# Attention's value products in quarters: one planner, two kinds of TensorE work, in a two-layer hybrid of convolution and attention

## The chip, the cores and the metric

The kernel runs on one core of one Trainium2 chip. The core has engines that work side by side, each on its own instruction queue: TensorE (PE, matrix products; its weight loads are listed apart as PEld), VectorE (DVE), ScalarE (ACT, here mostly exponentials), GpSimd (POOL) and SyncE (SP, which issues the transfers). An engine takes its instructions in the order in which they were written for it and waits, where it must, on semaphores that the others raise. The metric is the device time of one execution in microseconds (us); the median of three runs counts.

## The reference

Four images of 64 x 64 positions with 128 channels go through two layers. Cut to what matters here:

```python
# layer 0: elu, two 3x3 convolutions, a gate, causal attention with 1 head
# (4 wide for queries and keys, 16 wide for values), residual sums
x = _L0_conv_ref(x, ...)
# layer 1, on tokens t = [4, 4096, 128]
q = (x @ wq).reshape(bsz, seqlen, 16, 8)          # k, v alike
scores = einsum('bqhd,bkhd->bhqk', q, k)
probs = softmax(scores)
attn = einsum('bhqk,bkhd->bqhd', probs, v)
h = x + attn @ wo
t = t + h + (silu(h @ w1) * (h @ w3)) @ w2         # x is a layernorm of t
t = t + top-2 of 8 experts of layernorm(t), weighted by a router
```

The attention of layer 1 is the bulk: 4 batches x 16 heads x 4096 x 4096 scores, an exponential of each, and the product of the exponentials with the values.

## The kernel before

**Steps and turns.** Attention of layer 1 is cut into *segments*: one batch, one group of four heads, one tile of 512 queries (`Segment`, L1340). A segment runs over 32 key tiles of 128 keys; one key tile is a *step* (`attention_step`, L910). A step has two halves. `scores()` issues four products on PE, one per head, each on its own 32 rows of the array, into two score tiles `s` in PSUM (three such tiles exist, L192), and two exponentials on ACT from `s` into tiles `e` (six exist, L188). `values(es)` issues four products of 9 output rows (the sum of the exponentials and the 8 value channels) by 512 queries, which add up in the one PSUM tile `acc` over the segment's key tiles. At the last key tile DVE copies `acc` to `at`, and SP writes it to DRAM. In the trace each of these fp32 products stands as two instructions, so that a step's values show as `x8`.

**The planner.** The main loop (from L1476) issues one step per *turn* and writes the order of every engine by hand: `InOrder` (L104) ties each instruction to the one before it on its engine. It keeps account of PE's time with a few prices in us:

```python
    EXPS, SCORES, VALUES, PIECE, AHEAD = 1.81, 0.43, 0.987, 0.446, 0.39
        left = ahead + EXPS - SCORES - (VALUES if len(undone) > 2 else 0.0)
        ahead = min(max(left, 0.0), AHEAD)
        finish(2)
```

`EXPS` is the time that a turn has (its two exponentials), `left` what PE has over. A turn first issues its scores (`do_step`, L289), then perhaps other work, and last the values that are two steps behind: the list `undone` holds the steps whose values are outstanding, and `finish(2)` (L293, L1521) issues the oldest until two are left. What is left over, up to `AHEAD`, is carried into the next turn.

**The other work of a turn** comes from two sources.

- *Fillers* (`insert`, L307, and `advance`, L298): generators that do all the rest of the network in small pieces, between attention's steps. `convolutions` (L529) and `first_attention` (L666) prepare the next batch; `second_operands` (L742) makes queries, keys and values of layer 1; `last_part` (L1087) does everything behind attention for one tile of 512 tokens (output product, feed-forward part, router, experts), 32 of them in all. A piece is mostly half of a product of 512 columns (`halves`, L374: 256 columns, four products of 32 rows), or two products of 128 columns. A generator yields a price and a word: "held" if the single PSUM bank `m` (L194) is only half written, "free" or "stop" otherwise. A second piece then ends the bank in the next turn, and DVE reads it.
- *DVE jobs* (`Beside`, L958): in each segment over all keys, key tile 20 gets its exponentials from DVE. A job issues four score products into the bank `m` (a `unit` each, L986), DVE works out a polynomial (`beside_work`, L1037) into tiles `ey`, and two half products of 256 queries (`half`, L1026) add the result to `acc`.

In the kernel before a turn takes at most one of these: a filler piece or a piece of a job, when `left` is at least `PIECE`, or when a credit for fillers (which spreads them over the steps that remain) or the job's due time asks for it. The first two turns of a segment take none (`quiet`). `dve_time` (L150) estimates when DVE reads the bank (`turn_at[0] + 1.1` for a tile in `m`), and the loop uses that estimate to see whether the bank is empty.

**The end.** When the steps are used up, `finish(0)` issues the values that are left, and `run_alone` (L1250) runs what is left of the fillers with the PSUM banks of the scores. The last of them is `last_part` of the last tile of the last batch: it can begin only when that tile's attention is written to DRAM. It reads it back through `operands` (L1051): the sums (`sums<-d_a`), the rest (`an<-d_a`), then after a reciprocal `d_r<-sums` and `per<-d_r`.

Of the kernel before, what the change touches and what calls it, by code (L numbers as in the profile page):

```python
# [15 lines left out]
P = 128  # L16
# [4 lines left out]
QB = 512  # L21
# [5 lines left out]
SLOT = 32  # L27
NSLOT = P // SLOT
# [4 lines left out]
NH1, HD1 = 16, 8  # L33
# [93 lines left out]
def fast_path(ctx: ExitStack, tc: tile.TileContext, a: dict, where: dict, out: bass.AP, verdict):  # L127
# [11 lines left out]
    turn_at, dve_at, pool_at, bank_at = [0.0], [0.0], [0.0], [0.0]  # L139
# [5 lines left out]
            took = 0.65 + 1.25e-3 * int(np.prod(aps[0].shape[1:]))  # L145
            pool_at[0] = max(pool_at[0], turn_at[0] + 0.5) + took

    power_at, before = [0.0], [None]

    def dve_time(name, args):  # L150

        aps = [x for x in args if hasattr(x, "shape")]

        def reads(prefix):
            return any(x.name.startswith(prefix) for x in aps[1:])

        from_bank = reads("m_") or any(x.name == "m" for x in aps[1:])
        in_sbuf = not any(x.space == bass.MemoryType.PSUM for x in aps)
        took = max(int(np.prod(x.shape[1:])) for x in aps[:2]) / 960.0
        if in_sbuf and name in ("tensor_scalar", "tensor_copy"):  # L160
            took *= 0.5
        took += 0.075
        if any(x.name == before[0] for x in aps[1:]):
            took += 0.117
        before[0] = aps[0].name
        begins = 0.0
        if from_bank:
            begins = turn_at[0] + 1.1
        elif reads("acc"):
            begins = turn_at[0] + 1.85  # L170
        elif reads("e_"):
            begins = turn_at[0] + 2.2
        elif reads("rs_") and name == "tensor_scalar":
            begins = power_at[0] + 1.3
        begins = max(dve_at[0], begins)
        if in_sbuf and begins < pool_at[0] - 0.2:
            took += 0.75
        dve_at[0] = begins + took
        if aps[0].name.startswith("ve_"):
            power_at[0] = dve_at[0]  # L180
        if from_bank:
            bank_at[0] = dve_at[0]
# [96 lines left out]
    acc = ps_o.tile([P, QB], FP, tag="acc", name="acc")  # L279
# [6 lines left out]
    steps_in, undone, fillers = [], [], []  # L286
    bank_held = [False]

    def do_step(step):  # L289
        scores, values = step  # L290
        undone.append((values, scores()))

    def finish(leave):  # L293
        while len(undone) > leave:
            values, es = undone.pop(0)
            values(es)

    def advance(part):  # L298

# [7 lines left out]
    def insert():  # L307

        while fillers:
            r = advance(fillers[0])  # L310
            if r is not None:
                return r[0]
            fillers.pop(0)
        return 0.0
# [519 lines left out]
    def first_step(c, r, qx0, sums, found):  # L834

        diagonal = r == c

        if diagonal and c > 0:
            place = [(0, 0, 0), (1, P, P), (0, QB, 2 * P), (1, QB, 3 * P)]
            spans = [(0, QB + 2 * P), (P, QB + P)]  # L840
        else:
            place = [(j % 2, (j // 2) * QB, 0) for j in range(NSLOT)]
            spans = [(0, 2 * QB)] * 2

        def scores():
            ss, es = [s_tile(), s_tile()], [e_tile(), e_tile()]
            for j in BY_TILE:
                half, lo, off = place[j]
                r_ = slice(j * SLOT, j * SLOT + n_row)
                pe.matmul(  # L850
                    ss[half][:, lo : lo + QB - off],
                    lhsT=kx0[r_, r, :].bitcast(FR),
                    rhs=qx0[r_, off:].bitcast(FR),
                    start=True,
                    stop=True,
                )
            for e, s, (lo, hi) in zip(es, ss, spans):
                act.activation(e[:, lo:hi], s[:, lo:hi], AF.Exp)
            parts = []
            for j, (half, lo, off) in enumerate(place):  # L860
                e = es[half][:, lo : lo + QB - off]
                if diagonal:
                    at = j * P - off
                    if at:
                        pool.memset(e[:, :at], 0.0)
                    dve.tensor_tensor(e[:, at : at + P], e[:, at : at + P], k_of["tri"], ALU.mult)
                parts.append((off, e))
            return parts

        def values(parts):  # L870
            if r == 0:
                sums.append(acc if alone[0] else m_tile())
            for j, (off, e) in enumerate(parts):
                pe.matmul(
                    sums[0][j * SLOT : (j + 1) * SLOT, off:],
                    lhsT=v0[:, 4 * r + j, :],
                    rhs=e,
                    start=r == 0,
                    stop=r == c,
                )  # L880
            if r == c:
                at = chunk("at0")
                dve.tensor_copy(at, sums[0])
                found.append(at)

        return scores, values


    def keys(d, g, quarter, place):
# [20 lines left out]
    def attention_step(b, seg, kt, place, qx, vg, part):  # L910
        g, c = seg.g, seg.c

        def scores():
            ss, es = [s_tile(), s_tile()], []
            for j in BY_TILE:
                r = slice(j * SLOT, (j + 1) * SLOT)
                pe.matmul(
                    ss[j % 2][:, (j // 2) * QB : (j // 2 + 1) * QB],
                    lhsT=kx[r, place * P : (place + 1) * P].bitcast(FR),
                    rhs=qx[r, :].bitcast(FR),  # L920
                    start=True,
                    stop=True,
                )
            for s in ss:
                e = e_tile()
                act.activation(e, s, AF.Exp)
                es.append(e)
            return es

        def values(es):  # L930
            if kt == seg.hi - 1:
                beside_rest(seg)
            for j in range(NSLOT):
                pe.matmul(
                    acc[j * SLOT : j * SLOT + 1 + HD1, :],
                    lhsT=vg[:, kt // 4, kt % 4, j, :],
                    rhs=es[j % 2][:, (j // 2) * QB : (j // 2 + 1) * QB],
                    start=kt == seg.lo,
                    stop=kt == seg.hi - 1,
                )  # L940
            if kt == seg.hi - 1:
                at = chunk("at1")
                if part:
                    dve.tensor_tensor(at, acc, part[0], ALU.add)
                else:
                    dve.tensor_copy(at, acc)
                to = scratch[b]["a"][c, g] if seg.hi == NT else scratch[b]["p"][g, c]
                sp.dma_start(out=to, in_=at)
                if seg.hi == NT and g == NG1 - 1:
                    fillers.append([last_part(b, c), LAST, (b, c), False])  # L950
                    last_parts_left[0] -= 1

        return scores, values


    beside_todo = []
# [86 lines left out]
    def beside_rest(seg):  # L1043
        for job in seg.jobs:
            while job.halves < 2:
                beside_work(1e9)
                job.piece()
# [270 lines left out]
    lo, hi = where["rfold"]  # L1318
# [51 lines left out]
    jobs = []  # L1370
    now, quiet = [0], [False]
# [86 lines left out]
    def spread_beside():  # L1458
# [5 lines left out]
    left = run_alone(  # L1464
        [st.conv, first_attention(0, st), second_operands_beside(0, st), fold_and_spread(), spread_beside()],
        lambda: st.second >= plan[0].n and len(spread_of) == 3 and not st.plain,
    )
# [5 lines left out]
    credit, waiting = 0.0, False  # L1473


    EXPS, SCORES, VALUES, PIECE, AHEAD = 1.81, 0.43, 0.987, 0.446, 0.39  # L1476
    ahead = 0.0
    while True:
        turn_at[0] += EXPS
# [21 lines left out]
            later = PREPARE * (B - len(batches)) + LAST * (last_parts_left[0] - 1)  # L1501
            rate = (sum(part[1] for part in fillers) + later) / max(40, sum(steps_left) - 160)
        credit = min(3.0, credit + rate)
        left = ahead + EXPS - SCORES - (VALUES if len(undone) > 2 else 0.0)
        free = bool(fillers) and fillers[0][3]
        turn = not quiet[0] and free and not waiting
        if turn:
            took = insert()
            credit -= took
            left -= took  # L1510
        can = [job for job in jobs if job.can() and (left >= PIECE or job.late())]
        empty = bank_held[0] or bank_at[0] <= turn_at[0] + 0.3 or batches[b].second < NQ
        if can and empty and not (quiet[0] or bank_held[0] or steps_in or waiting):
            can[0].piece()
            left -= PIECE
        elif not turn and (waiting or not quiet[0] and empty and credit > 0.0 and (left >= PIECE or credit > 1.5)):
            took = insert()
            credit -= took
            left -= took
        ahead = min(max(left, 0.0), AHEAD)  # L1520
        finish(2)  # L1521
        for job in jobs:
            job.step()
        beside_work(turn_at[0] + 2.9, any(job.age > 3 * job.units + 4 for job in jobs if job.halves < 2))
# [720 lines left out]
```

## Time and profile before

| what | value |
|---|---|
| runs | 7981.13, 7985.75, 7992.59 us; median 7985.75 |
| profiled execution, its own time | 7983.82 us |
| its span, first to last instruction | 7982.0 us |
| TensorE clock granted, mean | 0.992 |
| first and last exponential of attention (start) | 71.6 and 7905.5 us |
| exponentials `e<-s` | 8256 |
| products `s<-qx,f_kx` of 512 columns, mean length | 495 ns |
| products `acc<-e,vg` of 512 columns, mean length | 594 ns |

The profile is one execution. A group line names the engine and operation, the tile written and those read, the shape, the count, then the busy time and the mean length of one, then the idle time before them and what ended it. On the timeline the first column is the start in us, the second how long the merged instructions lasted together. Products on PE are pipelined: a bar reaches into the next ones, so that the distance between starts, not the length, says how long PE was taken. Share of span in the chain of waits that ended last:

```profile
PE 87%; issue 7%; DVE 3%; ACT 1%; DMA 1%; POOL 1%; SPq 0%; ACTq 0%; DVEq 0%; POOLq 0%
PE acc L114 42%; PE s L114 26%; PE m L114 18%; DVE ey L114 1%; ACT e L114 1%; DVE h L114 0%; SPq L114 0%; DVE t L114 0%; DMA blocks<-d_y 0%; DMA f_kx<-d_k 0%; DVE em L114 0%; DVE pos L114 0%; DVE at L114 0%; POOL rs L114 0%; DVE c L114 0%
```

All instructions stand under L114, the line of the helper that records them; they are told apart by their tiles.

### The profile page before, as it was taken

To read this page: it belongs to the slowest core of one execution; us is meant where nothing else is said; L and a number is where in the kernel's file an instruction comes from. 1 tells how busy PE (TensorE), PEld (TensorE's weight loads), DVE (VectorE), ACT (ScalarE), POOL (GpSimd) and SP (SyncE) were. 2 spreads that over 40 slices of the span, in tenths; PEclk is the share of its full clock that TensorE was granted. 3 is DMA by queue.
4 is the path that set the end of the run, shared out by engine and by line. 5 is a ranking of instruction groups with operands and counts; after the bars stand their busy time and mean duration, and the time that the engine had idled before them with its cause. 6 is when DMAs were issued, how large, how long until landed. Compare 5 with 4: busy or idle time off the path is not lost.

```text
span 7982.0 us, 177748 instructions
## 1 busy us (share of the span) xinstructions
PE 7822.9 (98%) x73601; PEld 2457.5 (31%) x73601; DVE 4810.9 (60%) x9289; ACT 7670.4 (96%) x8459; POOL 676.4 (8%) x592
## 2 busy tenths in 40 slices
PE   7999999999999999999999999999999999999998
PEld 3232232332332323333332323333333333333333
DVE  4333556463666766665657766665666666666666
ACT  1899999999999999999999999999999999999996
POOL 1201211000012110000002111000000000000000
PEclk9999999999999999999999999999999999999998
DMA  2221010111110111111010111111111111111221
GB/s 73 67 69 68 22 60 30 61 35 59 35 31 13 51 39 45 33 38 37 28 35 25 34 32 39 51 43 33 32 31 50 51 51 50 54 49 51 68 72 42
DMA packets 332343, 356.58 MB, mean 45 GB/s; under 512 B 146083, under 2 KB 222339, under 8 KB 331523
## 3 DMA queue, kind: packets, MB, share of 16 engines
q1 hardware_dynamic: 327507, 343.35, 13.8%
q8 instruction: 579, 9.49, 0.5%
q10 hardware_dynamic: 4016, 1.77, 0.1%
q14 instruction: 241, 1.97, 0.1%
HBM read 209.24 MB, written 135.79 MB: 43 GB/s over the span
## 4 chain that ended last, share of the span: by engine, by line
PE 87%; issue 7%; DVE 3%; ACT 1%; DMA 1%; POOL 1%; SPq 0%; ACTq 0%; DVEq 0%; POOLq 0%
PE acc L114 42%; PE s L114 26%; PE m L114 18%; DVE ey L114 1%; ACT e L114 1%; DVE h L114 0%; SPq L114 0%; DVE t L114 0%; DMA blocks<-d_y 0%; DMA f_kx<-d_k 0%; DVE em L114 0%; DVE pos L114 0%; DVE at L114 0%; POOL rs L114 0%; DVE c L114 0%
## 5 line engine op out<-in xcount | busy, mean ns | idle before, releaser
L114 ACT ACTIVATE e<-s 128x1024 f32<-128x1024 f32 x8256 | 7608.8, 1097 | 101.3 <-PE s L114 97.2
L114 PE MATMUL acc<-e,vg 128*9 128x512 f32 x31872 | 4220.1, 594 | 0.6 <-DVE at L114 0.5
L114 PE MATMUL s<-qx,f_kx 32*128 32x512 f32 (+1 forms) x16512 | 2659.5, 495 | 38.7 <-DMA f_kx<-d_k 19.2
L114 PEld LDWEIGHTS s<-qx,f_kx 32*128 32x128 f32 (+1 forms) x16512 | 1084.7, 181 | 3862.1 <-ACT e L114 3633.7
L114 PEld LDWEIGHTS acc<-e,vg 128*9 128x9 f32 x31872 | 727.0, 90 | 799.7 <-issue 407.1
L114 DVE SCALAR_TENSOR_TENSOR ey<-ey,eg 128x512 f32<-128x512 f32 x1344 | 949.5, 706 | 33.1
L114 PE MATMUL m<-v,f_wino 128*32 128x256 f32 x5376 | 430.9, 392 | 12.8 <-POOL v L114 7.3
L114 DVE COPY at<-acc 128x512 f32<-128x512 f32 x131 | 90.6, 691 | 549.3 <-PE acc L114 546.0
L114 DVE TENSOR_SCALAR ey<-m 128x512 f32<-128x512 f32 x448 | 308.0, 688 | 85.7 <-PE m L114 71.0
L114 DVE SCALAR_TENSOR_TENSOR ey<-ey,em 128x512 f32<-128x512 f32 x448 | 323.4, 722 | 10.7
L114 DVE TENSOR_TENSOR by_e<-m,gates 128x512 f32<-128x512 f32 x240 | 165.0, 688 | 272.3 <-PE m L114 268.9
L114 DVE SCALAR_TENSOR_TENSOR eg<-em,ey 128x512 f32<-128x512 f32 x448 | 315.0, 703 | 9.4
L114 POOL TENSOR_TENSOR rs<-ve,f_minus_half 128x4 f32<-128x4 f32 x64 | 65.2, 1019 | 2967.6 <-DVE ve L114 2967.6
L114 DVE SCALAR_TENSOR_TENSOR ey<-eg 128x512 f32<-128x512 f32 x448 | 308.0, 687 | 0.0
L114 PE MATMUL m<-f_we,y2T 128*32 128x256 f32 x3840 | 306.7, 391 | 0.0
L114 POOL TENSOR_TENSOR v<-r 128x1024 f32<-128x1024 f32 x112 | 217.9, 1951 | 997.8 <-PE m L114 997.3
L114 DVE COPY sd<-m 128x512 f32<-128x512 f32 x168 | 116.0, 691 | 271.7 <-PE m L114 271.1
L114 POOL TENSOR_TENSOR t<-t,h 128x512 f32<-128x512 f32 x32 | 50.2, 1569 | 2240.3 <-DVE h L114 2240.3
L114 PE MATMUL m<-hT,f_fw 128*32 128x256 f32 (+1 forms) x2728 | 236.1, 391 | 0.4
L114 DVE TENSOR_TENSOR t<-m,t 128x512 f32<-128x512 f32 x61 | 42.2, 692 | 275.0 <-PE m L114 275.0
L114 DVE TENSOR_SCALAR em<-ey 128x512 f32<-128x512 f32 x448 | 197.2, 440 | 14.0
L114 DVE TENSOR_SCALAR em<-em 128x512 int32<-128x512 int32 x448 | 195.8, 437 | 11.1
(260 smaller groups left out, 4384.8 us busy)
## 6 DMA issues: line engine op xcount, KB each, us to landing
f_kx<-d_k SPq DMA_DIRECT2D x139, 512.0 KB
qx<-d_q SPq DMA_DIRECT2D x152, 256.0 KB
d_q<-two SPq DMA_DIRECT2D x64, 512.0 KB
d_a<-at SPq DMA_DIRECT2D x128, 256.0 KB
vg<-d_v SPq DMA_DIRECT2D x32, 576.0 KB
d_k<-two SPq DMA_DIRECT2D x32, 512.0 KB
d_v<-vc SPq DMA_DIRECT2D x32, 288.0 KB
xe<-in_x_dram SPq DMA_DIRECT2D x32, 256.0 KB
```

The lines of the kernel that those rows point to most:

```text
L114: made = op(*args, **kw)
```

## The change

The values of a step become divisible. `attention_step` returns a third item, `early`, and its `values` takes a range of quarters: columns `begin * 128` to `end * 128` of the 512 queries, for all four heads. The first step of a segment stays whole, and the last step's quarters may go early only when the segment's DVE job has done both its halves. `undone` counts quarters (4 for a step), and `add_values` issues as many as it is asked for.

A turn now issues at its end the quarters beyond eight (`must`), and after them, while `left` holds the price of a quarter and more than six quarters are outstanding, single quarters of the oldest step: up to two, half of a step's values. The prices are new: scores 0.54, a quarter 0.218, a job's unit 0.23 (`HEAD`), and 0.2 at most is carried over. Every job may place a piece in a turn, not the first alone; a turn may hold two filler pieces where the first leaves the bank half written and `left` holds the second; and DVE's estimated start is shifted by the first one's price (`shift`). The order of scores, other work and values within a turn is as before.

```diff
@@ dve_time
-            begins = turn_at[0] + 1.1
+            begins = turn_at[0] + 1.1 + shift[0]
@@
     def do_step(step):
-        scores, values = step
-        undone.append((values, scores()))
+        scores, values, split = step
+        undone.append([values, scores(), 4, split])
+
+    def add_values(quarters):
+
+        while quarters > 0:
+            values, es, left, split = undone[0]
+            some = min(left, quarters) if split else left
+            values(es, *((4 - left, 4 - left + some) if split else ()))
+            quarters -= some
+            undone[0][2] -= some
+            if some == left:
+                undone.pop(0)
+
+    def behind():
+        return sum(step[2] for step in undone)
 
     def finish(leave):
-        while len(undone) > leave:
-            values, es = undone.pop(0)
-            values(es)
+        add_values(sum(step[2] for step in undone[: max(0, len(undone) - leave)]))
@@ attention_step
-        def values(es):
-            if kt == seg.hi - 1:
+        def values(es, begin=0, end=4):
+            if kt == seg.hi - 1 and begin == 0:
                 beside_rest(seg)
+            lo, hi = begin * P, end * P
             for j in range(NSLOT):
                 pe.matmul(
-                    acc[j * SLOT : j * SLOT + 1 + HD1, :],
+                    acc[j * SLOT : j * SLOT + 1 + HD1, lo:hi],
                     lhsT=vg[:, kt // 4, kt % 4, j, :],
-                    rhs=es[j % 2][:, (j // 2) * QB : (j // 2 + 1) * QB],
+                    rhs=es[j % 2][:, (j // 2) * QB + lo : (j // 2) * QB + hi],
                     start=kt == seg.lo,
-                    stop=kt == seg.hi - 1,
+                    stop=kt == seg.hi - 1 and end == 4,
                 )
-            if kt == seg.hi - 1:
+            if kt == seg.hi - 1 and end == 4:
                 at = chunk("at1")
...
-        return scores, values
+        def early():
+            return kt < seg.hi - 1 or all(job.halves == 2 for job in seg.jobs)
+
+        return scores, values, early if kt > seg.lo else None
@@ main loop
-    EXPS, SCORES, VALUES, PIECE, AHEAD = 1.81, 0.43, 0.987, 0.446, 0.39
+    EXPS, SCORES, VALUES, PIECE, HEAD, AHEAD = 1.81, 0.54, 0.218, 0.446, 0.23, 0.2
...
-        left = ahead + EXPS - SCORES - (VALUES if len(undone) > 2 else 0.0)
-        free = bool(fillers) and fillers[0][3]
-        turn = not quiet[0] and free and not waiting
-        if turn:
+        must = max(0, behind() - 8)
+        left = ahead + EXPS - SCORES - VALUES * must
+        took, beside = None, False
+        if not quiet[0] and fillers and fillers[0][3] and not waiting:
             took = insert()
             credit -= took
             left -= took
-        can = [job for job in jobs if job.can() and (left >= PIECE or job.late())]
         empty = bank_held[0] or bank_at[0] <= turn_at[0] + 0.3 or batches[b].second < NQ
-        if can and empty and not (quiet[0] or bank_held[0] or steps_in or waiting):
-            can[0].piece()
-            left -= PIECE
-        elif not turn and (waiting or not quiet[0] and empty and credit > 0.0 and (left >= PIECE or credit > 1.5)):
+        for job in jobs:
+            cost = HEAD if job.units < NSLOT else PIECE
+            if job.can() and empty and (left >= cost or job.late()):
+                if not (quiet[0] or bank_held[0] or steps_in or waiting):
+                    job.piece()
+                    left -= cost
+                    beside = True
+        for n in range(1 if waiting else 2):
+            if took is None:
+                go = waiting or not (quiet[0] or beside) and empty and credit > 0.0
+                go = go and (waiting or left >= PIECE or credit > 1.5)
+            else:
+                go = took > 0.0 and bank_held[0] and left >= PIECE
+            if not go:
+                break
+            shift[0] = 0.0 if took is None else took
             took = insert()
+            shift[0] = 0.0
             credit -= took
             left -= took
+        add_values(must)
+        while left >= VALUES and behind() > 6 and undone[0][3] and undone[0][3]():
+            add_values(1)
+            left -= VALUES
         ahead = min(max(left, 0.0), AHEAD)
-        finish(2)
```

Layer 0's attention steps (`first_step`, L834) return `None` as their third item and stay whole. Each output element is the same sum; only the place at which a DVE job's key tile is added among the others can differ. Neither a tile nor a buffer is added.

## The prediction

> **What bounds the kernel now.** I read the page first (busy time, the chain of waits), then the timeline of single engines.
>
> ```profile
> span 7982.0 us, 177748 instructions
> ...
> PE 7822.9 (98%) x73601; PEld 2457.5 (31%) x73601; DVE 4810.9 (60%) x9289; ACT 7670.4 (96%) x8459; POOL 676.4 (8%) x592
> ...
> L114 ACT ACTIVATE e<-s 128x1024 f32<-128x1024 f32 x8256 | 7608.8, 1097 | 101.3 <-PE s L114 97.2
> ```
>
> Two engines are nearly full at once. ACT's exponentials are the work nobody else can take; PE feeds them. The idle 101.3 us before the exponentials understate the loss, since a busy bar includes an exponential's latency. Pace tells more. The timeline of ACT alone:
>
> ```profile
> 6399.23 16.62 ACT L114 ACTIVATE e<-s 128x1024 f32<-128x1024 f32 x18
> 6415.49 0.46 ACT L114 ACTIVATE pr<-lg 128x32 f32<-128x32 f32 x1
> 6415.61 63.14 ACT L114 ACTIVATE e<-s 128x1024 f32<-128x1024 f32 x68
> 6478.63 0.63 ACT L114 ACTIVATE th<-h 128x512 f32<-128x512 f32 x1
> ```
>
> 18 exponentials take 6415.49 - 6399.23 = 16.26 us, 0.903 each: ACT's own pace, 1.806 for a turn's two. The 68 behind them take 63.02 us, 0.927 each: there ACT waits a little in every turn. Over the whole trace the 7,993 distances from one full exponential to the next hold 203 us above 0.903: 85.7 us in 3,341 distances of 0.915 to 0.96, 34 in 249 of 0.96 to 1.2, 81 in 57 longer ones. The first band is what a smoother PE could win back. PE's timeline shows its cause:
>
> ```profile
> 6405.61 0.70 PE L114 MATMUL s<-qx,f_kx 32*128 32x512 f32 x4
> 6406.24 1.04 PE L114 MATMUL acc<-e,vg 128*9 128x512 f32 x8
> 6407.22 0.92 PE L114 MATMUL s<-qx,f_kx 32*128 32x512 f32 x4
> ...
> 6411.73 0.43 PE L114 MATMUL m<-y2T,f_rw 128*32 128x128 f32 x8
> 6411.98 0.61 PE L114 MATMUL acc<-e,vg 128*9 128x512 f32 x4
> ```
> ```profile
> 6444.73 0.50 PE L114 MATMUL s<-qx,f_kx 32*128 32x512 f32 x4
> 6445.16 0.64 PE L114 MATMUL m<-f_we,y2T 128*32 128x256 f32 x8
> 6445.62 1.04 PE L114 MATMUL acc<-e,vg 128*9 128x512 f32 x8
> 6446.59 0.51 PE L114 MATMUL s<-qx,f_kx 32*128 32x512 f32 x4
> 6447.03 0.62 PE L114 MATMUL acc<-ey,vg 128*9 128x256 f32 x8
> 6447.46 1.04 PE L114 MATMUL acc<-e,vg 128*9 128x512 f32 x8
> 6448.43 0.50 PE L114 MATMUL s<-qx,f_kx 32*128 32x512 f32 x4
> ```
>
> Starts, not lengths, give prices. Scores 0.43 to 0.44; a filler half 0.46 (6445.16 to 6445.62); values 0.97 up to the next scores. The 256-wide half step takes 0.43 (6447.03 to 6447.46), so whole values are 0.86 and 0.11 is the change from values to scores. A turn with a filler is 6446.59 - 6444.73 = 1.86, 0.054 over ACT's 1.806; one with a DVE job's half 1.84, 0.034 over; one without either 1.405, and PE waits (its scores stretch from 0.50 to 0.92).
>
> **The change, part by part.** I cut both orders of PE's instructions into turns (scores to scores) and counted. Before: 2,217 turns with a filler half (or two 128-wide products) and whole values, 222 with a DVE job's half, 448 with one of its score products ("unit"), 1,235 without.
>
> *Removed: long unbroken runs.* A run of filler or half turns starts with the lead that PE has gained and then loses 0.054 a turn. Counting all turns beyond the second of a run gives 1,455 x 0.054 = 79 us (beyond the first 101, beyond the third 64), close to the measured 85.7: the lead is worth two such turns, 0.11 us. The changed order has 574 such turns: 31 us. Gain 47.6 (with the other two readings 48 and 43).
>
> *Added: turns filled by quarters.* 258 turns hold two filler halves and two quarters (0.44 + 0.91 + 0.43 + 0.11 = 1.89, 0.084 over), 344 a unit and five quarters (scores and a unit take 0.66, 6468.72 to 6469.38; 0.66 + 1.075 + 0.11, 0.04 over), 233 six quarters (1.84, 0.034 over). At most 22 + 14 + 8 = 44 us. Each needs less than the lead of 0.11, and stands behind a turn with time left; only those that follow each other pay. I take a quarter, and keep 0 and all of it.
>
> *Added: narrow groups.* The columns streamed stay the same; 15,048 matrix products more are issued (45,493 to 60,541), in 3,752 more groups of four, each with its own weight loads. No 128-wide product on nine columns is in the trace. Lower bound: none beyond its columns, 0.215 a quarter. Upper: a lone 128-wide product on 32 columns, 0.25 (6411.73 to 6411.98), 0.035 more. Nearest is the DVE job's half on the same nine columns: start to start the two passes average 0.436 against 0.430 for half a whole step. I take 0.008 more, 0.223. Of the groups 941 lie in filler and half turns: 941 x 0.008 = 7.5 us; 1,387 in the unit and six-quarter turns above, which raises their 44 to 55, a quarter of it 14; the rest lie in turns where PE waits, hidden by that wait of up to 0.40.
>
> The Trainium skill speaks against this part: "TensorE: Matmul & The Clock Gate", section "Back-to-back issue gap", states about 81 ns per product sustained at 128 columns and 131 at 512, so that a quarter costs 62% of a whole. By that each of the 3,752 groups would add 0.32 us to its 0.215, 1,200 us in all, an estimate from that page's ratio. The row of 128-wide products on the output weights contradicts it here: 16 of them start at 6467.29 and the next work at 6467.75, 0.029 each.
>
> Loop: -47.6 + 7.5 + 14 = **-26 us**. Ends: -48, and +78 (941 x 0.035 = 33, plus 44 + 49 uncovered, less 48).
>
> *Moved: the last part of tile 6 of the last batch.* DVE instructions are otherwise the same but for one transposition; SP issues five DMAs more (that part's turn through DRAM, now under the loop). SP's queue at the end:
>
> ```profile
> 7908.39 0.33 SPq L114 DMA_DIRECT2D d_a<-at  x1
> 7914.63 0.32 SPq L114 DMA_DIRECT2D d_g<-turned  x1
> 7916.21 2.90 SPq L114 DMA_DIRECT2D g<-d_g  x4
> 7919.21 0.58 SPq L114 DMA_DIRECT2D sums<-d_a  x1
> ```
>
> The very last attention result leaves at 7908.39, but its read (sums) stands behind four gate reads of the part before, at 7919.21. In the changed order that part's experts are done before the last exponential; only its bias product is left. The read then waits for the write alone, 1.5 (as d_g) to 3.0 us (as d_r, in the chain): 7.8 to 9.3 us earlier. What follows is a serial chain. I take **-8** (0 if DMAs collide).
>
> Earlier values also release e tiles and copy acc sooner; nothing waits there (0.6 us before acc products), so nothing is gained. The one new wait is a quarter whose exponential has not ended; scores of the next turn queue behind it. At the earliest it starts 0.44 + 0.43 = 0.87 behind the scores, about the 0.903 of the exponential that it needs, and only where PE has time left: zero; without that cover, 0.05 a turn, and the next turn's scores are late by as much.
>
> **Sum.** Profiled execution 7983.8 - 26 - 8 = 7950; the median lies 1.9 above that execution: **7952 us**.
>
> **Rivals.** *Quarters too dear (slower).* A narrow group pays as the lone 128-wide one does, 0.25. Filler turns pay 33, the heavy turns 93, of which half uncovered since the lead of 0.11 no longer holds: 33 + 46 - 48 - 8 = +23, 8009. Break-even is 0.236 a quarter, slower by 0.2% from 0.245. For it: 40% more PE instructions; against it: the nine-column half's 0.436. *No change, heavy turns uncovered:* the planner counts on a lead of 0.2 where runs show 0.11; 55 + 7.5 - 48 - 8 = +6, 7992. Against it: a heavy turn needs the turn before it to be light. *No change, DVE late:* two halves in one turn use the single m bank in another rhythm; one wait such as acc for ey at 4889.60 costs 2.1 us, and 15 new ones take back 32: 7984. For it: the 57 distances above 1.2 are of this kind; against it: DVE is 60% busy. *The order does not change:* excluded by the counts.
>
> **How the numbers follow.** Forecast 0.58, the two no-change rivals 0.22 together, quarters too dear 0.20. About 0.2% (16 us) is what a measurement can tell. Faster 0.60, same 0.19, slower 0.21 (a few of each rival cross over). The forecast's own range is 7928 (-48, -9) to 7970; the 8-in-10 range goes to 7922, for long gaps that may shrink, and to 8004, short of the dear quarters' 8009.
>
> **What would show it.** A quarter's start-to-start of 0.22 (0.25 would be the first rival); the 0.915-0.96 band down from 85.7 to about 45; ACT's 68 exponentials in that stretch nearer 62.3 than 63.0; sums<-d_a about 3 us behind d_a<-at. A count of longer gaps grown by fifteen would make the forecast wrong through DVE, an unchanged band through the heavy turns.

## The result: 0.05% faster, not to be told from no change

| | median of 12 runs | lowest to highest | profiled execution | its span |
|---|---|---|---|---|
| before | 7983.36 us | 7975.94 to 7992.59 | 7983.82 us | 7982.0 us |
| after | 7979.90 us | 7973.55 to 7984.37 | 7979.66 us | 7977.8 us |

After against before: 0.9995, 95% interval 0.9986 to 1.0004. The forecast of 7952 had 34 us of gain in it (26 in the loop, 8 at the end), the chip shows 3.5. The page after, its span and busy lines and the two groups that the change touches (columns as before):

```profile
span 7977.8 us, 237947 instructions
...
PE 7760.0 (97%) x103701; PEld 3280.2 (41%) x103701; DVE 4798.3 (60%) x9289; ACT 7661.9 (96%) x8459; POOL 671.5 (8%) x592
...
L114 ACT ACTIVATE e<-s 128x1024 f32<-128x1024 f32 x8256 | 7600.4, 1113 | 111.2 <-PE s L114 106.6
L114 PE MATMUL acc<-e,vg 128*9 128x128 f32 (+3 forms) x61880 | 4278.8, 387 | 1.9 <-DVE at L114 1.8
```

PE's instructions grew from 73,601 to 103,701, and its busy time fell by 63 us; but ACT, whose exponentials set the end, sat idle before them for 111.2 us, 10 more than before. PE's new leisure did not reach ACT. ACT's timeline of the stretch that the prediction showed:

```profile
6421.77 0.42 ACT L114 ACTIVATE pr<-lg 128x32 f32<-128x32 f32 x1
6421.89 62.95 ACT L114 ACTIVATE e<-s 128x1024 f32<-128x1024 f32 x68
6484.61 0.74 ACT L114 ACTIVATE th<-h 128x512 f32<-128x512 f32 x1
```

The same 68 exponentials take 6484.61 - 6421.89 = 62.72 us, where 63.02 were before and 61.4 would be ACT's own pace.

SP's queue at the end, after:

```profile
7912.82 0.33 SPq L114 DMA_DIRECT2D d_a<-at  x1
7913.88 0.39 SPq L114 DMA_DIRECT2D out_dram<-t  x1
7914.87 0.57 SPq L114 DMA_DIRECT2D sums<-d_a  x1
```

The read of the last sums now goes out 2.05 us behind the write of the attention result, 10.82 before. This part did what was forecast.

**Where the time went.** I gave the loss of every turn (the distance from its first exponential to the next turn's, less 1.806 and less ACT's other work in between) to what PE had in that turn, by the order of its instructions. Losses of 0.8 us and more stand apart: there PE waits for a late result of DVE or a transfer. All from the two profiled executions, in us:

| part | before | after | difference |
|---|---|---|---|
| up to the first exponential | 71.6 | 74.6 | +2.9 |
| turns with one filler piece | 102.2 in 2,125 | 57.2 in 1,636 | -44.9 |
| heavy turns (two pieces and two quarters; unit and five quarters; six quarters) | none | 17.7 in 258; 16.9 in 344; 8.1 in 231 | +42.7 |
| all other turns | 37.6 | 29.6 | -8.0 |
| losses of 0.8 and more | 91.0 in 25 | 100.7 in 28 | +9.7 |
| behind the last exponential's start | 76.5 | 68.2 | -8.3 |

The rows make -5.9 against -4.2 between the spans (the rest lies in turns with other shapes). The first row is the same program in both and tells how far two executions differ. So filler turns won what was forecast, heavy turns paid it back, and the end gave its 8 us. Of the -8.0 of the other turns nearly all lies in 92 turns with a piece of four 128-by-128 products: beside four quarters it overran (11.7 us before), and after the change most of them hold three quarters beside it (3.2 us).

**Why the heavy turns pay.** PE's timeline after, columns as before:

```profile
6428.30 0.86 PE L114 MATMUL s<-qx,f_kx 32*128 32x512 f32 x4
6429.09 1.07 PE L114 MATMUL m<-f_we,y2T 128*32 128x256 f32 x16
6429.98 0.61 PE L114 MATMUL acc<-e,vg 128*9 128x256 f32 x8
6430.52 0.51 PE L114 MATMUL s<-qx,f_kx 32*128 32x512 f32 x4
6430.96 1.48 PE L114 MATMUL acc<-e,vg 128*9 128x512 f32 x24
6432.38 0.50 PE L114 MATMUL s<-qx,f_kx 32*128 32x512 f32 x4
6432.81 1.07 PE L114 MATMUL m<-f_we,y2T 128*32 128x256 f32 x16
6433.69 0.61 PE L114 MATMUL acc<-e,vg 128*9 128x256 f32 x8
6434.24 0.51 PE L114 MATMUL s<-qx,f_kx 32*128 32x512 f32 x4
```

Two pieces with two quarters, then six quarters, then two pieces with two quarters: scores follow scores after 1.86 us, 0.05 over ACT's 1.806, in the second and the third of these turns (6430.52 to 6432.38 to 6434.24). They do follow each other: of 831 heavy turns 561 stand right behind another turn that is over 1.806, 386 of them behind another heavy one, for behind a turn that has taken two quarters in advance, the next one has only two left to issue, and the planner fills it with a second piece. Lead can be read from the trace. In a turn in which ACT waits, the first exponential starts 0.59 us behind the start of the turn's last score products; what it starts later than that is PE's lead. The measure holds: a filler turn that begins with none loses 0.057 before and 0.061 after in the median, one that begins with 0.05 to 0.1 loses 0.001 and 0.003. Of 802 heavy turns whose neighbours hold no other ACT work, 57% begin with no lead (under 0.012), their median is 0.006, and 73% make ACT wait. The planner's own `ahead`, which comes out as the program is built, has a median of 0.137 in front of the same turns.

Here is why it has not got what it counts:

```profile
6441.57 0.51 PE L114 MATMUL s<-qx,f_kx 32*128 32x512 f32 x4
6442.01 0.64 PE L114 MATMUL m<-f_we,y2T 128*32 128x256 f32 x8
6442.47 0.83 PE L114 MATMUL acc<-e,vg 128*9 128x256 f32 x16
6443.23 0.60 PE L114 MATMUL s<-qx,f_kx 32*128 32x512 f32 x4
6443.76 0.64 PE L114 MATMUL m<-f_we,y2T 128*32 128x256 f32 x8
6444.22 1.05 PE L114 MATMUL acc<-e,vg 128*9 128x384 f32 x16
6445.19 0.51 PE L114 MATMUL s<-qx,f_kx 32*128 32x512 f32 x4
```

A turn with a filler and three quarters takes 1.66 (6441.57 to 6443.23), so that 0.146 should be left. But its successor's scores stretch to 0.60: the first two products start at 6443.23, the last two at 6443.33. They wait for the score tile that the turn's first exponential (6442.17) is still reading; there are three such tiles. In both traces the last two score products of an undisturbed turn start at least 1.08 us behind that exponential's start, with few exceptions. The lead can so be at most 1.806 - 1.08 - 0.59 = 0.14 (0.15 behind a turn in which ACT waited, which takes 1.82), and here it is 0.075, since the last two start 1.16 behind the exponential and not 1.08. What delays them beyond 1.08 the traces don't show. Medians over turns that began with none: 0.15 behind a plain light turn (1.40 us) before the change; after it 0.07 to 0.08 behind a filler with three quarters or behind five quarters. A filler turn takes 0.05 to 0.06 of it, so that 0.07 covers one of them. The change fills exactly the turns that gave 0.15: plain light turns fell from 1,008 to 531. And two turns, 0.11 us, is more than lead covered even before the change. Asked by a turn's place in its run, the trace of before has the first filler turn begin with a lead of 0.073 and lose 0.010 (medians of 414 undisturbed turns), the second begin with 0.002 and lose 0.045 (318 turns), and later ones lose 0.05 to 0.06. The count beyond the second turn, 79 us, came near the band's 85.7 by coincidence: filler turns alone lost 102.2, near the 101 of the count beyond the first.

One sum would have warned. Priced from the traces (0.54 for scores with the change of layout, 0.445 a piece, 0.2175 a quarter, 0.225 a unit, 0.425 a job's half, 0.006 a further group, other pieces at what they take there), all turns together run over 1.806 by 159 us in the old order, in 2,437 turns, and by 155 in the new, in 2,499. Lead covered 20 of the one and 26 of the other.

### The profile page after: what moved, and what is told of

It reads as the page before. It is cut to its first block, busy times and chain, and to the rows that moved or that the text cites. A ratio compares the mean times of both kernels' runs of the same rounds, so it can differ in the third digit from the quotient of the medians.

```text
span 7977.8 us, 237947 instructions
## 1 busy us (share of the span) xinstructions
PE 7760.0 (97%) x103701; PEld 3280.2 (41%) x103701; DVE 4798.3 (60%) x9289; ACT 7661.9 (96%) x8459; POOL 671.5 (8%) x592
## 4 chain that ended last, share of the span: by engine, by line
PE 44%; issue 2%; DVE 2%; ACT 2%; DMA 0%; POOL 0%; SPq 0%; ACTq 0%; DVEq 0%; POOLq 0%
PE acc L114 22%; PE s L114 13%; PE m L114 9%; ACT e L114 1%; DVE ey L114 1%; DVE h L114 0%; DVE em L114 0%; DVE t L114 0%; DVE eg L114 0%; DVE by_e L114 0%; DMA blocks<-d_y 0%; SPq L114 0%; POOL rs L114 0%; DVE f_c_band L114 0%; DVE c L114 0%
## 5 line engine op out<-in xcount | busy, mean ns | idle before, releaser
L114 ACT ACTIVATE e<-s 128x1024 f32<-128x1024 f32 x8256 | 7600.4, 1113 | 111.2 <-PE s L114 106.6
L114 PE MATMUL acc<-e,vg 128*9 128x128 f32 (+3 forms) x61880 | 4278.8, 387 | 1.9 <-DVE at L114 1.8
L114 PE MATMUL s<-qx,f_kx 32*128 32x512 f32 (+1 forms) x16512 | 2556.8, 495 | 88.7 <-ACT e L114 56.4
L114 PEld LDWEIGHTS acc<-e,vg 128*9 128x9 f32 x61880 | 1562.0, 90 | 1777.6 <-issue 1209.5
L114 PEld LDWEIGHTS s<-qx,f_kx 32*128 32x128 f32 (+1 forms) x16512 | 1049.1, 182 | 2068.4 <-ACT e L114 1337.7
```

What stands on the lines that cost most here:

```text
L114: made = op(*args, **kw)
```

## Experiments

The theory after the result was that heavy turns spend a lead that PE has not got, and pay in full. The rivals: narrow groups cost too much; two pieces in a turn and DVE's later reads make the long gaps. Each run stands beside runs of the kernel before on its chip: 7983.72 us (e1 to e4), 7982.46 (e5 to e8), 7984.10 (e9 to e12), medians of 20 to 32. "Short" are losses under 0.8 us, "long" those above, summed as in the table (before: 139.8 and 91.0; after: 129.5 and 100.7).

**e1. Quarters at the old place.** The kernel before; each step's values but a segment's first as four quarters, where the whole stood.

```diff
-            for j in range(NSLOT):
-                pe.matmul(acc[..., :], ..., rhs=es[j % 2][...])
+            for n, w in enumerate(widths):      # four slices of 128 columns
+                for j in range(NSLOT):
+                    pe.matmul(acc[..., w], ..., rhs=es[j % 2][...])
```

> The kernel before, with every step's values (but a segment's first) issued as four quarters at the old place: nothing moves, some 11,600 more groups of four products. If a narrow group costs the 0.006 us that the changed kernel's sections show, PE has 70 us more to do; the part that lies in turns without spare time shows: 8010 to 8055. If a narrow group is dear (0.035, the lone 128-wide product), 400 us more work: 8200 to 8400.

8013.15 us, 1.0037 (1.0022 to 1.0051): cheap groups; the dear ones are refuted. A filler turn on e1's PE timeline:

```profile
6471.95 0.51 PE L114 MATMUL s<-qx,f_kx 32*128 32x512 f32 x4
6472.39 0.64 PE L114 MATMUL m<-f_we,y2T 128*32 128x256 f32 x8
6472.84 1.06 PE L114 MATMUL acc<-e,vg 128*9 128x128 f32 x32
6473.83 0.51 PE L114 MATMUL s<-qx,f_kx 32*128 32x512 f32 x4
```

Values to the next scores take 0.99 (6472.84 to 6473.83) where a whole step took 0.97: 0.006 for each of three more groups.

**e2. No quarters early.** The changed kernel without its early quarters; the rest of the change stays.

```diff
-        while left >= VALUES and behind() > 6 and undone[0][3] and undone[0][3]():
-            add_values(1)
-            left -= VALUES
```

> The changed kernel without the loop that issues quarters early; new prices, several pieces per turn and the rest stay. Theory of the heavy turns (PE's usable lead is about one overrun of 0.05, so turns filled by early quarters pay in full what the shorter runs win): the short losses go back to what they were before, about 140 us, and the tail's 8 us may be lost as well: 7985 to 8005. Theory of late DVE reads (two halves in one turn and other job pieces make long gaps): long gaps stay near 100 us. Theory of dear narrow groups: 20 us or more faster than the changed kernel, under 7960.

8025.23, 1.0053 (1.0036 to 1.0070). A miss. Behind the last exponential 99.7 us pass instead of 68.2, because fillers no longer find room in time and are left over; the loop has short losses of 144.7, its filler turns 103.6 as in the kernel before. So the shorter filler runs need the early quarters; without them the new prices only push fillers to the end.

**e3. One piece in a turn.**

```diff
-        for n in range(1 if waiting else 2):
+        for n in range(1):
```

> The changed kernel with at most one filler piece in a turn. Heavy turns: the 258 turns with two pieces pay 18 us now; without them the same pieces stand in turns of their own, so little changes, within 5 us of the changed kernel's 7980. Late DVE reads: long gaps fall from 101 us back to 91, some 10 us faster, 7970.

7990.99, 1.0010 (1.0001 to 1.0020): 11 above the changed kernel, outside of what both expected. Turns lose 124.0 in short (5.5 less) and 111.2 in long losses (10.5 more): the long ones are not made by two pieces, which speaks against that rival. The short ones are an exchange: heavy turns lose 14.5 instead of 42.7, one-piece filler turns 82.4 instead of 57.2. And 7.6 of the 11 lie at the end, 75.8 us instead of 68.2: only the second pieces bring the last fillers under the loop.

**e4. A carried lead of 0.12.**

```diff
-    EXPS, SCORES, VALUES, PIECE, HEAD, AHEAD = 1.81, 0.54, 0.218, 0.446, 0.23, 0.2
+    EXPS, SCORES, VALUES, PIECE, HEAD, AHEAD = 1.81, 0.54, 0.218, 0.446, 0.23, 0.12
```

> The changed kernel with 0.12 carried over at most, not 0.2. Heavy turns: the planner spends less lead that PE has not got, fewer turns of five and six quarters and of two pieces overrun; short losses fall by about 20 us from 129: 7955 to 7965. Late DVE reads, dear groups: no change beyond 5 us, 7975 to 7985.

7970.91, 0.9985 (0.9975 to 0.9994): the theory's direction, half its size. The heavy turns lose 22.0 instead of 42.7, the one-piece filler turns 74.6 instead of 57.2. It is nearly an exchange: all short losses together fall by some 4 us, and as much of the gain lies in the long ones.

**e5. The end alone.** The kernel before with one number changed:

```diff
-            rate = (...) / max(40, sum(steps_left) - 160)
+            rate = (...) / max(40, sum(steps_left) - 210)
```

> The kernel before, with one number of its planner changed: the fillers are spread so that they end 210 steps before the last instead of 160. Nothing of quarters, nothing of two pieces in a turn; the aim is the order of the last stretch alone, in which the last part of tile 6 ends under the loop as it does after the change. The first theory (the tail's 8 us have nothing to do with quarters): the stretch behind the last exponential falls from 76.5 to about 68 us, the loop stays within 2 us, together 7974 to 7978. The rival (the tail is shorter because early quarters bring the last attention result forward): the stretch stays at 76 and the time at 7983.

7977.47, 0.9995 (0.9986 to 1.0004), the stretch behind the last exponential 68.2 us. SP's queue in e5:

```profile
7905.47 0.33 SPq L114 DMA_DIRECT2D d_a<-at  x1
7907.49 0.57 SPq L114 DMA_DIRECT2D sums<-d_a  x1
```

2.02 us from write to read, as after the change. The rival, that early quarters bring the end forward, is refuted. One number of the planner gives as much as the whole change, without a quarter, and like the whole change it can't be told from nothing by the time alone.

**e6. Quarters only into their own turn's room.** The changed kernel, in which early quarters may not use the carried lead.

```diff
-        while left >= VALUES and behind() > 6 and ...
+        while left - ahead >= VALUES and behind() > 6 and ...
```

> The changed kernel, but a quarter is moved forward only into room that its own turn has, not into lead carried over from the turns before; fillers and halves still use the lead. The turns of six quarters and of a unit with five quarters are gone (none of 231 and 344 left), 676 turns hold five quarters, and 1,779 instead of 1,343 turns hold a filler half and whole values. First theory (the lead PE really has is worth about half a heavy turn, 0.03 us, so those heavy turns paid in full): by that lead the turns lose 122 us instead of 131: 7968 to 7974. Rival (the lead of 0.11 of the prediction, heavy turns mostly covered): 86 instead of 69, so 16 us slower, about 7995.

7965.93, 0.9979 (0.9970 to 0.9988). The time is as the theory said, 30 us below the rival; but the reason is not its own. Short losses are 134.0, not fewer than the changed kernel's 129.5: the heavy turns with quarters are gone (25.0 less), filler turns with one piece lose 29.4 more. These 575 turns neither won nor cost more than 4.5 us. In the profiled execution the gain stands in the long losses, 82.2 in 19 instead of 100.7 in 28.

**e7. Prices as in the trace.** The planner's constants 1.806, 0.55, 0.2225, 0.46, 0.23, 0.1, and fillers that end 300 steps before the last.

```diff
-    ... = 1.81, 0.54, 0.218, 0.446, 0.23, 0.2
+    ... = 1.806, 0.55, 0.2225, 0.46, 0.23, 0.1
@@
-            rate = (...) / max(40, sum(steps_left) - 160)
+            rate = (...) / max(40, sum(steps_left) - 300)
```

> The changed kernel with the planner's prices as the trace has them (1.806 for a turn's exponentials, 0.55 for scores with the change of layout, 0.2225 for a quarter, 0.46 for a piece), a carried lead of at most 0.1, and fillers that end 300 steps before the last, so that the tail stays as it is after the change. First theory (usable lead 0.03): turns lose 110 us instead of 131, so about 7959, 7952 to 7966. Rival (lead 0.11): 72 instead of 69, no change against the changed kernel, 7980 to 7986. Third theory (late DVE work makes the long gaps): depends on them alone; 76 turns with two pieces and three quarters stay, so within 5 us of 7980.

7973.76, 0.9988 (0.9979 to 0.9997): between the theories. Short losses are 129.4, the same as after the change, where 110 was expected for a usable lead of 0.03. One number for the lead does not carry over to other orders; e6 and this run refute that form of the theory.

**e8. A carried lead of 0.39.** `AHEAD` as before the change.

```diff
-    EXPS, SCORES, VALUES, PIECE, HEAD, AHEAD = 1.81, 0.54, 0.218, 0.446, 0.23, 0.2
+    EXPS, SCORES, VALUES, PIECE, HEAD, AHEAD = 1.81, 0.54, 0.218, 0.446, 0.23, 0.39
```

> The changed kernel with a carried lead of up to 0.39, the value before the change, in place of 0.2: 435 turns with two pieces and two quarters instead of 258, 418 with six quarters instead of 231, 646 plain light turns instead of 531. First theory (a lead that the planner counts and PE has not got is paid back in full): turns lose 188 us instead of 131, about 8035. Rival (carried lead is real, the ring of score tiles holds it): no loss, 7970 to 7985. Third theory (two pieces in a turn make DVE late): the loss stands in gaps above 0.8 us, 15 or more of them beyond the 28.

8015.45, 1.0043 (1.0028 to 1.0058): 36 us above the changed kernel, two thirds of what the theory asked. Short losses 155.3 (+26), of which 34.0 in 134 turns with two pieces and three quarters, 0.25 each; long ones 113.0 in 38 (+12). So most of a lead that is only counted is paid for.

**e9. The first exponential's products first.**

```diff
-            for j in range(NSLOT):
+            for j in BY_TILE:                  # 0, 2, 1, 3
                 pe.matmul(acc[...], ...)
```

> The changed kernel with the four products of every values pass in another order: the two that read the turn's first exponential before the two that read its second (0, 2, 1, 3 instead of 0, 1, 2, 3). In the trace after the change 757 values stretches of the form half, quarter, quarter take 1.031 us instead of 0.982 in three of four cases, since the second product of the first early quarter waits for the second exponential and holds the two behind it. Theory (those turns have 0.3 us left, so that wait costs nothing): within 5 us of the changed kernel's 7980. Rival (it delays the scores behind it): up to 757 x 0.05 = 38 us faster, 7942 to 7965.

7979.14, 0.9994 (0.9985 to 1.0003): no change. But the edit did not take the wait away. The stretches of half, quarter, quarter still take 1.026 us in the median (1.031 before the edit, 0.982 where nothing waits), so this run does not test whether the wait is covered. It is also rarer than the expectation has it: 457 of the 757 stretches after the change, three in five, take over 1 us. The loss by turns after the change has to stand in: 528 plain turns with values in three groups lose 0.009 us each, as plain turns did before (0.010); 59 turns with a job's half lose 0.049 where 89 of them with whole values lose 0.032, 1.0 us in all.

**e10 and e11. e6 and the changed kernel with another placement.** Both with 210 in place of 160, as in e5.

> e6 again with another order of the work: a quarter goes forward only into its own turn's room, and the fillers are spread to end 210 steps before the last instead of 160, which shifts most fillers by a turn or a few. It tells whether e6's gain against the changed kernel lies in what it undoes or in a lucky place of a few late DVE results (its gaps of 0.8 us and more hold 82 us in 19, the changed kernel's 101 in 28). Theory (heavy turns that stand behind a late DVE result lengthen its gap): gaps stay below 88 us and the time is 7962 to 7970. Rival (luck): gaps of 92 to 105 us and 7975 to 7985.

> The control to e10: the changed kernel with its fillers spread to end 210 steps before the last, nothing else. The classes of turns stay nearly as they are (1,401 filler turns with whole values, 333 of a unit and five quarters, 209 of six quarters, 230 of two pieces and two quarters). Theory (gaps belong to the heavy turns): gaps of 95 to 106 us, time 7976 to 7984. Rival (luck of place): gaps anywhere from 82 to 105 us, and with them the time from 7962 to 7984.

e10: 7975.85, 0.9990 (0.9981 to 0.9999); e11: 7979.93, 0.9997 (0.9988 to 1.0006). Short losses repeat: 131.2 against e6's 134.0, 127.6 against 129.5. Long ones do not: e10 has 97.6 in 28 where e6 had 82.2 in 19; e11 has 106.6 in 31. Against the kernel before on its chip e6 won 16.5 us and e10 8.3: half of e6's gain is a lucky placement of the fillers. At this second placement the rule itself gives the 4.1 us between e10 and e11, whose intervals overlap.

**e12. e6 and e9 together.**

> e6 and e9 together, as the version that the runs so far point to: quarters only into their own turn's room, and the products of the first exponential first. If the wait for the second exponential is covered, as e9 is to show, the same as e6: 7961 to 7970; if it is paid, up to 275 x 0.05 = 14 us less, 7950 to 7958.

7964.35, 0.9976 (0.9967 to 0.9986): as e6, and the lowest median of all, 0.2% below both kernels of the study. Its turns are in e6's order, and its long losses are 92 us in 24, against 82.2 in 19, in a profiled execution 6 us above its median. So long losses of single executions differ by some 10 us even at one placement, and the comparisons of them above are no finer than that.

**What a long loss is.** PE's timeline at the same place of the work, first before, then after; the bracket is idle time and what ended it:

```profile
1397.32 0.61 PE L114 MATMUL acc<-ey,vg 128*9 128x256 f32 x6
1399.85 0.38 PE L114 MATMUL acc<-ey,vg 128*9 128x256 f32 x1 [1.92 <-DVE ey L114]
```
```profile
1395.76 0.61 PE L114 MATMUL acc<-ey,vg 128*9 128x256 f32 x6
1398.47 0.60 PE L114 MATMUL acc<-ey,vg 128*9 128x256 f32 x1 [2.09 <-DVE ey L114]
```

In both a DVE job's half waits about 2 us for its last `ey`. ACT loses 2.8 us before, 4.3 after. The windows behind the two waits, before and then after (from and to, length, busy time and count of PE, PEld, DVE, ACT and POOL, then the granted TensorE clock, the transfers' share, GB/s):

```profile
1399.80:1402.00 2.20, 2.15 (x22) 0.71 (x26) 0.00 (x0) 0.00 (x0) 0.00 (x0) 1.00 0.62 97
```
```profile
1398.40:1401.10 2.70, 2.63 (x26) 1.17 (x26) 0.72 (x2) 0.00 (x0) 0.00 (x0) 0.51 0.01 1
```

After, the granted clock is 0.51 behind the wait, before it is 1.00. The trace has the clock halved for 3.41 us from 1398.45 on, and the passes of a quarter (four 128-wide products side by side, two passes a quarter) follow each other there by 0.21 to 0.22 us in place of 0.109. Not every such wait does it: 1.92 here and 2.11 at 4889.6 in the trace of before leave the clock alone, 2.09 at 2968 halves it. From 400 us to the last exponential the clock is halved for 27.3 us in the trace of before, 37.5 after, 68.3 in e3, 51.2 in e11, 23.9 in e5, 30.7 in e6; the long losses of these are 91.0, 100.7, 111.2, 106.6, 86.8 and 82.2. In the other eight traces the two go together less closely (41.0 halved and 92 lost in e12, 34.1 and 113.0 in e8). In each of the fourteen traces all halved stretches begin on one grid of 3.41 us, and the grid lies elsewhere in each trace. The wait after the change falls into one step of its grid (2.08 us), that before into two (1.22 and 0.70), which fits the pair; but at 4889.6 before 2.02 us fell into one step and the clock stayed whole, so that the grid alone does not give the rule. The Trainium skill's "TensorE: Matmul & The Clock Gate", section "Part 1: The HAM clock gate (the "warmup" mystery)", tells of half the clock after an idle window of about 3.4 us, with windows that run freely. The 3.41 us agree and the grid speaks for free windows; but here a wait of 2.09 us was enough. That the clock makes the whole difference of +9.7 was not isolated by a run: 10.2 us more at half the clock are worth some 5 by estimate, and less where PE idles in them.

## Why the prediction was wrong in size, step by step

The 7979.9 lies in the 8-in-10 range (7922 to 8004) but above the forecast's own (up to 7970): of 34 us of gain 3.5 are seen, which can't be told from none. In number it stands nearest to the rival of late DVE results (7984), but that is luck: it asked for fifteen more long waits, and there were three.

- **Long unbroken runs, -47.6: right.** Filler turns with one piece lose 44.9 less, where the sum had 40 with the 7.5 for groups. The three readings of the lead gave 43 to 48, so that the wrong one, two turns, did no harm here.
- **Turns filled by quarters, "I take a quarter": the step that failed.** The sum had 14 for them with their groups; they lost 42.7, close to the upper end of 44. The reason given was that each needs less than a lead of 0.11 and "stands behind a turn with time left; only those that follow each other pay". But two in three stand behind another turn over 1.806, which the order of instructions would have told before the run, and 57% begin with no lead; and the lead of 0.11 was itself too large, 0.073 in front of a run before the change and 0.07 to 0.08 behind a turn that a quarter has filled. Of the 42.7, 30.0 lie in turns behind another full one, the rest in those behind a lighter one, whose median loss is 0.004. This is the mechanism of the rival that named heavy turns uncovered (7992); it lies 12 above the result, chiefly since it left out the 8.0 that other turns gained and its 55 was above the 42.7, against which stand the 9.7 of long losses.
- **Narrow groups, 7.5: right to high.** A further group takes 0.005 to 0.006 (0.977 for three quarters and one against 0.972 for whole values, 501 and 858 stretches), where 0.008 was taken; e1 shows that even 11,600 groups cost only some 30 us. The Trainium skill's "TensorE: Matmul & The Clock Gate", section "Back-to-back issue gap", has figures by which a quarter would cost 62% of a whole, as an estimate. The trace does not agree: the four products of a 128-wide pass start 0.109 us behind the four before, two passes a quarter, 25% of the 0.86.
- **The end, -8: right**, measured 8.3. e3 shows that the second pieces are what brings it, and e5 that it needs neither these nor quarters.
- **The early quarter's wait on its exponential, "zero": nearly right.** The wait exists, about 0.05 us in three of five of the 757 stretches, and most of it lies in turns with time left; where a job's half takes that time, it cost 1.0 us.
- **Long gaps, nothing in the sum:** +9.7 us, three more events, where the rival asked for fifteen. Placement, and even another execution of one order, moves them by as much.

By the signs it had named: the quarter's price held (0.2175); the band of 0.915 to 0.96 fell only to 73.7 where 45 was forecast, which it said would show the heavy turns.

What stays open: how much of the long losses' 9.7 belongs to the change; and why short losses in e6 and e7 did not fall although the sum of their overruns did (140 and 138 against 155). Their light turns are refilled more often (239 and 369 plain ones left of 531), which would lower the lead; no run isolates it.

## What to carry to other kernels

Where two engines are both nearly full, sum the overruns of all turns in both orders, at full price, before granting any of them cover: moving work from one full turn into another that it fills moves the loss along. Count also how many of the filled turns stand behind another full one. The sum is a warning and no forecast: in e6 and e7 it fell by 15 us and more, and the loss did not follow. Lead counted by a planner is worth no more than the ring of buffers lets the leading engine take, so read it from the trace, as start distances, behind just the kind of turn that is to refill it. And look for what one constant of the old kernel would give before crediting a large rewrite with it.

## What was not expected of the hardware

A wait of 2 us on PE can cost up to 1.7 more, an estimate from 3.41 us at half the clock: the pair above lost 4.3 and 2.8. Which waits halve the clock, the runs don't settle. When ACT has had to wait for the first of a turn's score tiles, the distance to its second exponential is 0.920 us, not 0.903, though the second tile's products began 1.5 us before it: so in 1,864 of 3,892 undisturbed turns before and 1,690 after. A 128-wide pass of four products on nine columns (0.109 us) runs at the streaming pace of a 512-wide one (0.43), while going from values to scores costs 0.11 us each turn, as much as half a quarter.
